# Interval constants over more steps, Newton steps in the quiet part of the weights' cycle, and images placed by eight transfers, in a kernel of three relu-difference convolutions

## The chip, the cores and the metric

The kernel runs on one core of a Trainium2 chip. The metric is the device time of one execution in microseconds (us). One execution was also taken by the hardware profiler; all times of single instructions below come from it.

## What is computed

The reference is a chain of four layers on x (4 images, 32 x 32 pixels, 16 channels, float32), each with a group norm in front and a sum behind it. Layers 0, 1 and 3 are the same convolution-like layer with their own weights, and layer 2 is a dynamic program over intervals:

```python
def conv(inputs, M, W, G):      # layers 0, 1, 3
    first = jnp.einsum('ijyx,byxc->bijc', Msq, inputs)
    shifted = ...               # a 3x3 convolution with own filters for each output pixel (i, j)
    diff = jax.nn.relu(inputs[:, None, None, :, :, :] - shifted)
    second = jnp.einsum('ijyx,bijyxc->bijc', Wsq, diff)
    return first - second

def intervals(a, ...):          # layer 2
    r = [interval_pooling(a, 'max'), interval_pooling(a, 'min')]
    f = dp_step(r, r, W0, b0)                      # max over k of sigmoid(f[i,k] Wf + r[k,j] Wr + b)
    f = dp_step([f, r], r, W1, b1)
    return sigmoid([f, r] @ W2 + b2)[:, :-1, 1:]

for layer in (conv0, conv1, intervals, conv3):
    x = x + layer(group_norm(x))
```

For each output pixel (i, j) and each filter, a whole image of 1024 pixels is convolved, cut at zero, and summed with the weights of that pixel. This is nearly all of the work.

## The kernel before, in words

**Phases and steps.** The four images are two pairs (g = 0, 1). A phase is one pair in one of the three convolution layers, in the order (0, 0), (1, 0), (0, 1), (1, 1), (0, 2), (1, 2), where the second number counts the convolutions. So phases alternate between the pairs, and what has to happen to one pair between two layers (norm, intervals, new operands) is done beside the matmuls of the other pair. A phase has 8 chunks of 128 output pixels, a chunk 16 filters x 2 images = 32 steps, so there are 256 steps in a phase and 1536 in all. One step (first_part and second_part, L678 and L702) is one filter of one image for 128 output pixels and 1024 image pixels:

- TensorE: matmuls into one pair of PSUM banks (L663). The float32 values are split into three parts, and the products of the parts are summed: first the products with ib and ia, then, after ScalarE has scaled the sum in place (L699), those with iyz and im. ia, ib, iyz and im9 are the operands made from the image.
- VectorE: minimum with zero times the weights WT, summed along the row (L716, into the tile junk). It is the last reader of the bank pair. There are four bank pairs, so TensorE starts on a pair again when the L716 of four steps earlier is done.

second_part of a step is issued after first_part of the step that follows. [...]the order is written out by hand, and no scheduler moves anything.

**The weights' cycle.** prep_parts (L221) is a generator that the conv loop calls once per step (`next(parts)`, L754). It prepares one unit (4 filters) of split weights in eight steps. Written by the step number modulo 8: at 1 VectorE makes the upper part (L204, tile upper_w); at 2 ScalarE takes a half for W9 (L176); at 3 GpSimd subtracts (L238) and adds (L239), ScalarE scales (L237); at 4 GpSimd adds and copies (L242, L244, L246) and ScalarE copies (L241); at 5 GpSimd subtracts the identity from the next unit (L215, prep), for which its raw weights must have landed; at 6 nothing; at 7 SyncE issues two transfers of parts (L252) and the load of the raw weights of the unit after the next (L111, 768 KB); at 0 nothing. What the generator yields says for what else a step is good: IDLE at 5, 6, 7, 0 and 1; CALM at 6, 7 and 0.

**What runs beside.** `behind` (L769) is the generator of everything else. The conv loop takes one stretch of it at a time: `yield n` asks for n steps until the next stretch, `yield IDLE` and `yield CALM` wait for a step of that kind (L763 to L765). Its order is:

- phase 0: rest_of_start (L905, the operands of the second image and the norm of the first pair), zeros(1), constants (L462: the mask and small weights of the interval layer, loaded as wv and written by GpSimd as blocks, L476, and the memset of rt, L483);
- phases 3 and 4, ahead of the last convolution of each pair and beside matmuls of the other: interval_layer (L501). It has its group norm (tile names with _i), four transposes (L530), scans (L549), the products left and right_side (L573, L588), and two dynamic steps which end with transfers of s to r, a part of tables (L632); left("l2") at L641 reads r after the last of them;
- then before_conv (L383): the group norm (tile names with _c), a transpose (L390), eight writes to the DRAM tile xs (L396), 24 reads into the tile raw (L407), the split of each of two images on GpSimd (L281) with ScalarE (L285), the half of im (L176), `place` (L291) with its transfers into ia (L299) and ib (L301) through SyncE's queue, and `difference` into iyz (L289);
- after the second pair of layers 0 and 1, and at the end: the first terms (L432).

The group norm (L334) takes sums on VectorE, with `gap` steps between its parts, and then has a block of small operations on GpSimd that follow one another: L326, three times L328 to L331 (Newton steps for an inverse root), and L376, which writes the normed values. They stand in GpSimd's queue between the weights' operations. The norm of the interval layer has gap 2; that of a conv 4, or 1 in the last layer.

**The operands.** temp holds both split parts, ty and tz, of both halves of both images. place copies quarters of it (32 partitions, L195) to the partitions that the matmuls need: per half, four transfers of 32 x 496 to ia and two of 32 x 512 to ib, so twelve for one image, ia ahead of ib.

Of the kernel before, what the change touches and what calls it, by code (L numbers as in the profile page):

```python
# [45 lines left out]
def net_kernel(ctx: ExitStack, tc: tile.TileContext, x, xq, xi, convs, iv_w, iv_b, out):  # L46
# [131 lines left out]
    def halve_rest(dst, src, mask):  # L178
        nc.vector.scalar_tensor_tensor(
            dst, src, mask[:, 0:1], dst.bitcast(F32), op0=ALU.mult, op1=ALU.add  # L180
        )
# [87 lines left out]
        halve_rest(units[u][3][:, at:to], raws[u][:, 2, at:to], low_p)  # L269

    def halves(temp, b):
        v = temp.rearrange("p (k s b n) -> p k s b n", k=2, s=2, b=GB)
        return v[:, 0, :, b], v[:, 1, :, b]

    def split(eng, g, b, temp, name, pause=IDLE):
# [11 lines left out]
    def difference(eng, g, b, s, temp):  # L287
        ty, tz = (v.bitcast(F32)[:, s] for v in halves(temp, b))
        eng.tensor_tensor(iyz[g][:, s, b], ty, tz, ALU.subtract)  # L289

    def place(g, b, temp):  # L291

        ty, tz = (v.bitcast(F32) for v in halves(temp, b))
        da, db = (v[g].bitcast(F32)[:, :, b] for v in (ia, ib))
        for h, (lo, hi) in enumerate(QUARTERS):
            for s in range(2):
                at = HW if s == h else 0
                for to, src in ((lo, ty), (hi, tz)):
                    nc.sync.dma_start(da[to, s, :LAST], src[lo, s, at : at + LAST])  # L299
            for to, src in ((lo, ty), (hi, tz)):  # L300
                nc.sync.dma_start(db[to], src[hi])  # L301
        yield 1


# [26 lines left out]
            nc.gpsimd.tensor_tensor(y, y, t, ALU.mult)  # L331
        return y

    def group_norm(g, name, dst, gap):  # L334


        def sums(src):
            nc.vector.tensor_reduce(
                part[:, : GC // 2], src.rearrange("p t (g s) -> p g t s", s=2), axis=AX.XY, op=ALU.add
            )  # L340

        def totals(name):

            turned = work.tile([P, 32], F32, tag="turned", name=f"turned_{name}")
            nc.vector.transpose(turned, part)
            by_quarter = work.tile([32, 4], F32, tag="by_quarter", name=f"by_quarter_{name}")
            for q in range(4):
                nc.vector.tensor_reduce(
                    by_quarter[:, q : q + 1], turned[32 * q : 32 * q + 32], axis=AX.X, op=ALU.add
                )  # L350
            yield gap
            total = work.tile([P, 32], F32, tag="total", name=f"total_{name}")
            for q in range(4):
                nc.vector.tensor_reduce(
                    total[32 * q : 32 * q + 32, 0:1], by_quarter, axis=AX.X, op=ALU.add
                )
            yield gap
            whole = work.tile([P, 32], F32, tag="whole", name=f"whole_{name}")
            nc.vector.transpose(whole, total[:, 0:1].to_broadcast([P, 32]))
            return whole[:, : GC // 2]  # L360

        sums(X[g])
        yield gap
        m = yield from totals(f"m{name}")
        mean = work.tile([P, GC // 2], F32, tag="mean", name=f"mean_{name}")
        nc.gpsimd.tensor_scalar_mul(mean, m, 1.0 / (2 * NP))
        xc = work.tile([P, NT, GC], F32, tag="xc", name=f"xc_{name}")
        nc.gpsimd.tensor_tensor(pair_view(xc), pair_view(X[g]), spread(mean), ALU.subtract)
        sq = work.tile([P, NT, GC], F32, tag="sq", name=f"sq_{name}")
        nc.gpsimd.tensor_tensor(sq, xc, xc, ALU.mult)  # L370
        yield 4
        sums(sq)
        yield gap
        v = yield from totals(f"v{name}")
        rstd = inverse_root(v, name)
        nc.gpsimd.tensor_tensor(pair_view(dst), pair_view(xc), spread(rstd), ALU.mult)  # L376
        yield 6

    xns = {}
    part = const.tile([P, 32], F32, name="part")  # L380
# [2 lines left out]
    def before_conv(g, layer):  # L383
        xn = work.tile([P, NT, GC], F32, tag="xn", bufs=2, name=f"xn_{g}_{layer}")
        xns[g] = xn
        yield from group_norm(g, f"c{g}{layer}", xn, 1 if layer == 2 else 4)

        nc.vector.transpose(  # L390
            xt[g][:, :, 1 : 1 + H], xn
        )
        inner = xs[g][:, :, WP : WP + H * WP].rearrange("p h (t r n) -> p h r t n", r=ROWS, n=WP)
        for r in range(ROWS):
            for h in range(2):
                nc.sync.dma_start(  # L396
                    inner[:, h, r], xt[g][GC * r : GC * (r + 1), :, HW * h : HW * h + WP]
                )
        yield 2
        xsv = xs[g].rearrange("(b c) h n -> c h b n", b=GB)  # L400
        for slot, row, tap in [
            (slot, row, tap) for slot in range(2) for row, tap in enumerate(TAPS[slot])
        ] + [(2, row, 8) for row in range(4)]:
            for h in range(2):
                off = tap // 3 * WP + tap % 3
                r0 = 64 * h + C * row
                nc.sync.dma_start(  # L407
                    raw[r0 : r0 + C, slot ^ h if slot < 2 else 2, :, :RUN], xsv[:, h, :, off : off + RUN]
                )
            yield 1  # L410
        yield 6 if layer == 2 else 12
        temp = big.tile([P, 8192], F32R, tag="big", name=f"temp_{g}{layer}")[:, :TEMP]
        for b in range(GB):
            yield from split(nc.gpsimd, g, b, temp, f"{g}{layer}")
            yield IDLE
            halve(image(im9[g][:, b], HW), image(raw[:, 2, b], WP), low_x)
            yield from place(g, b, temp)
            for s in range(2):
                difference(nc.gpsimd, g, b, s, temp)
            yield 1  # L420
            halve_rest(image(im9[g][:, b], HW), image(raw[:, 2, b], WP), low_x)
            yield 4

    def load_first_terms(layer):
        mt = big.tile([P, NT, 4, 256], F32, tag="big", name=f"MT_{layer}")
# [36 lines left out]
    def constants():  # L462
# [18 lines left out]
            )  # L481

        nc.gpsimd.memset(rt, 0.0)  # L483
        yield 1


        for k, hidden, name in ((0, None, "f0"), (3, 2, "f1"), (6, 5, "f2")):
# [7 lines left out]
        for k, name in ((1, "r0"), (4, "r1")):  # L495
            t = const.tile([P, NQ * GB, C], F32, name=name)
            for q in range(NQ):
                blocks(t[:, q * GB : (q + 1) * GB, :], k, mask2, GB)
            iv[name] = t.rearrange("p k c -> p (k c)")
            yield 1  # L500
    def interval_layer(g):  # L501

        R = 2 * GC
# [19 lines left out]
        yield 1  # L523
        nc.gpsimd.memset(r[:R, :, 0:1], 0.0)
        nc.gpsimd.memset(r[:R, H:], 0.0)
        yield from group_norm(g, f"i{g}", xi, 2)

        raw = one[:GC].rearrange("p (j t r) -> p r t j", j=H, r=ROWS)
        for row in range(ROWS):
# [108 lines left out]
        yield from right_side("r1", iv["r1"])  # L638
        ftp = left("l1", iv["f1"])
        yield from step("b", ftp, bv[:, 1:2])  # L640
        z = left("l2", iv["f2"])  # L641
        y = ivp.tile([P, QI, H], F32, tag="y", name=f"y_{g}")
        nc.scalar.activation(y, z[:, :, 1:], AF.Sigmoid, bias=bv[:, 2:3])
# [125 lines left out]
    def behind(phase):  # L769
        g, layer = phases[phase]  # L770
        if phase == 0:
            yield from rest_of_start()
            nc.sync.dma_start(X[1], x[1])
            zeros(1)
            yield 1
            yield from constants()
        if phase + 1 < len(phases):
            g1, layer1 = phases[phase + 1]
# [126 lines left out]
    def rest_of_start():  # L905
# [12 lines left out]
        halve_rest(image(im9[0][:, 1], HW), image(raw[:, 2, 1], WP), low_x)  # L918
        prep_plain_rest(1)
        yield 2  # L920
        temp = first.bitcast(F32R)[:, used : used + TEMP]
        for b in range(GB):
            yield from split(nc.vector, 0, b, temp, "00", 1)
            yield from place(0, b, temp)
# [91 lines left out]
```

## Time and profile before

| what | value |
|---|---|
| median of 3 runs | 2479.14 us (2476.86 to 2479.35) |
| the profiled execution | 2478.91 us |
| its span on the core | 2477.1 us |
| L716, VectorE | 1536 of 1224 ns, with 83 ns more to read the sum |
| L699, ScalarE | 1520 of 1008 ns |
| L238, L239, L242, GpSimd | 190 each of 1300 ns |
| L215, GpSimd | 190 of 1052 ns |
| raw weights, L111 | 190 transfers of 768 KB, 7.1 us to landing |
| ia from temp, L299 | 80 transfers of 62 KB, 5.6 us to landing |
| ib from temp, L301 | 40 transfers of 128 KB, 4.4 us to landing |

PE is TensorE's matmuls, PEld its weight loads, DVE is VectorE, ACT ScalarE, POOL GpSimd and SP SyncE. A line of a timeline has the start in us, the duration in us, the engine, the line of the kernel, the operation, what is written and read with partitions x elements, and in brackets how long the engine had been idle before it and who ended that. A line of the waits has who waited for whom, the sum in us, how often, and the longest.

### The profile page before, as it was taken

The page shows a single profiled execution, that of the slowest core. Times are in us where ns is not written, and L with a number is a line of the kernel's source. Part 1 is how long each engine was busy: PE and PEld are TensorE (multiplying, and loading weights), DVE is VectorE, ACT ScalarE, POOL GpSimd, SP SyncE. Part 2 cuts the span into 40 slices and gives each one's busy share as a digit, 9 for nine tenths or more (in the row PEclk, how much of TensorE's full clock was granted, in tenths as well). Part 3 has the DMA queues.
Part 4 walks back from the last instruction along what each step waited for, and adds up shares of the span by engine and source line. Part 5 has one row for each costly group of instructions (what it writes and reads, how often), then busy time and mean ns, then how long its engine had stood idle before and what let it go on. Part 6 is the DMA issues. An engine that isn't in the chain of part 4 may idle for free. (4 is left out here: it accounts for less than half of the span.)

```text
span 2477.1 us, 58166 instructions
## 1 busy us (share of the span) xinstructions
PE 2457.9 (99%) x21906; PEld 2072.9 (84%) x21906; DVE 2077.0 (84%) x3637; ACT 1871.4 (76%) x2159; POOL 1589.7 (64%) x1857
## 2 busy tenths in 40 slices
PE   8999999999999999999999999999999999999999
PEld 5998888888888888888888898888889888888887
DVE  9888878888888888878888888888888888788887
ACT  3778767787777778767777777777777787677776
POOL 4767545676565667555567776776777675555552
PEclk9999999999999999999999999999999999999999
DMA  6457654475444467644454454674445476554442
GB/s 198 128 156 191 188 144 134 131 195 149 135 142 137 137 168 194 190 112 136 137 145 129 126 142 132 174 171 130 129 135 141 119 197 186 154 148 137 137 137 54
DMA packets 97674, 366.92 MB, mean 148 GB/s; under 512 B 26480, under 2 KB 31472, under 8 KB 97392
## 3 DMA queue, kind: packets, MB, share of 16 engines
q1 hardware_dynamic: 96832, 362.79, 53.5%
q8 instruction: 172, 2.82, 0.5%
q14 instruction: 110, 0.90, 0.1%
q10 hardware_dynamic: 432, 0.39, 0.0%
q0 software_dynamic: 128, 0.02, 0.0%
HBM read 199.78 MB, written 1.02 MB: 81 GB/s over the span
## 5 line engine op out<-in xcount | busy, mean ns | idle before, releaser
L716 DVE SCALAR_TENSOR_TENSOR junk<-pc,WT 128x1024 f32<-128x1024 f32 x1536 | 1879.6, 1224 | 353.5 <-PE pc L663 303.8
L699 ACT ACTIVATE pc<-pc 128x1024 f32<-128x1024 f32 x1520 | 1532.2, 1008 | 563.8 <-PE pc L663 530.4
L663 PE MATMUL pc<-ib,parts 64*128 64x512 f32 x6080 | 950.2, 388 | 4.3 <-DVE junk L716 3.0
L663 PE MATMUL pc<-iyz,parts 64*128 64x512 f32 x6080 | 947.2, 387 | 2.3 <-ACT pc L699 1.6
L663 PE MATMUL pc<-ia,parts 64*128 64x496 f32 x6080 | 924.8, 379 | 0.0
L663 PEld LDWEIGHTS pc<-ib,parts 64*128 64x128 f32 x6080 | 582.4, 184 | 109.8 <-DVE junk L716 9.6
L663 PEld LDWEIGHTS pc<-ia,parts 64*128 64x128 f32 x6080 | 585.4, 184 | 106.0
L663 PEld LDWEIGHTS pc<-iyz,parts 64*128 64x128 f32 x6080 | 583.5, 184 | 92.6 <-ACT pc L699 7.3
L663 PE MATMUL pc<-im,W 64*128 64x496 f32 x3072 | 603.2, 384 | 0.0
L238 POOL TENSOR_TENSOR parts<-raw,upper_w 128x512 fp32r<-128x512 f32 x190 | 247.0, 1300 | 497.6 <-DVE upper_w L204 413.1
L663 PEld LDWEIGHTS pc<-im,W 64*128 64x128 f32 x3072 | 296.6, 184 | 56.9 <-issue 3.4
L244 POOL CAST parts<-parts 32x512 fp32r<-32x512 f32 x380 | 231.6, 609 | 39.3 <-ACT parts L241 20.8
L242 POOL TENSOR_TENSOR parts<-parts 128x512 fp32r<-128x512 f32 x190 | 247.0, 1300 | 1.6 <-ACT parts L237 1.5
L246 POOL CAST parts<-upper_w 32x512 fp32r<-32x512 f32 x380 | 233.1, 613 | 22.8
L239 POOL TENSOR_TENSOR W<-W,raw 128x512 fp32r<-128x512 f32 x190 | 247.4, 1302 | 0.4 <-ACT W L176 0.3
L215 POOL TENSOR_TENSOR raw<-raw,ident 128x512 f32<-128x512 f32 x190 | 199.8, 1052 | 73.7 <-DMA raw<-in_g 45.8
L176 ACT ACTIVATE W<-raw,low_w 128x512 fp32r<-128x512 f32 x190 | 136.2, 717 | 1.7 <-DMA raw<-in_g 1.6
L716 DVE DVE_READ_ACCUMULATOR junk<-pc,WT 128x1 f32 x1536 | 127.9, 83 | 0.0
L237 ACT ACTIVATE parts<-upper_w 128x512 fp32r<-128x512 f32 x190 | 118.9, 626 | 7.7 <-DVE upper_w L204 7.5
L241 ACT CAST parts<-upper_w 128x512 fp32r<-128x512 f32 x190 | 116.4, 613 | 0.0
L731 POOL TENSOR_SCALAR acc<-acc 128x32 f32<-128x32 f32 x40 | 15.6, 391 | 136.8 <-DVE junk L716 134.7
L204 DVE TENSOR_SCALAR upper_w<-raw 128x512 int32<-128x512 int32 x190 | 82.4, 433 | 19.0 <-POOL raw L215 18.6
(152 smaller groups left out, 470.4 us busy)
## 6 DMA issues: line engine op xcount, KB each, us to landing
raw<-in_g SPq DMA_DIRECT2D x190, 768.0 KB, 7.1
parts<-parts SPq DMA_DIRECT2D x380, 384.0 KB, 5.0
WT<-in_w SPq DMA_DIRECT2D x48, 512.0 KB, 4.7
MT<-in_mt SPq DMA_DIRECT2D x24, 512.0 KB, 7.3
raw<-xs SPq DMA_DIRECT2D x120, 71.8 KB, 4.1
ib<-temp SPq DMA_DIRECT2D x40, 128.0 KB, 4.4
ia<-temp SPq DMA_DIRECT2D x80, 62.0 KB, 5.6
ib<-first SPq DMA_DIRECT2D x8, 128.0 KB, 2.4
```

The lines of the kernel that those rows point to most:

```text
L176: nc.scalar.activation(dst, src, AF.Copy, scale=mask[:, 1:2])
L215: eng.tensor_tensor(raws[u][:, s, at:to], raws[u][:, s, at:to], pick[s][:, f0 + at : f0 + to].unsqueeze(2).to_broadcast([P, to - at, P]), ...
L237: nc.scalar.activation(WD, high, AF.Copy, scale=-EPS)
L238: nc.gpsimd.tensor_tensor(WL, w8, high, ALU.subtract)
L239: nc.gpsimd.tensor_tensor(W9, W9.bitcast(F32), src[:, 2], ALU.add)
L241: nc.scalar.copy(WU, high)
L242: nc.gpsimd.tensor_tensor(WD, WD.bitcast(F32), WL.bitcast(F32), ALU.add)
L244: nc.gpsimd.tensor_copy(WU[hi], WL[lo].bitcast(F32))
L246: nc.gpsimd.tensor_copy(WL[lo], high[hi])
L663: nc.tensor.matmul(ps[:, h, at : at + n], lhsT=w[r], rhs=v[r] if n == NH else v[r][:, :n], start=first and k == 0, stop=k == len(pairs) - ...
L699: nc.scalar.activation(ps, ps, AF.Copy, scale=1.0 + EPS)
L716: nc.vector.scalar_tensor_tensor(junk, ps.rearrange("p h n -> p (h n)"), 0.0, chunks[n], op0=ALU.min, op1=ALU.mult, accum_out=accs[phase][ ...
```

## The change

The kernel after differs in four places.

- **place and its position.** One image is placed by eight transfers: the four to ib first (32 x 2 x 512, as before), then four to ia (32 x 2 x 496), each for both halves at once; they read temp through a view with a pitch, for which temp is now the whole tile. In before_conv the order is now split, half of im, difference, two steps, rest of im, two steps, place. Before, place came right behind the half of im.
- **constants.** Six steps instead of one ahead of them, four instead of one after the memset of rt, and a step after each of the blocks of r0 and r1. What follows in phase 0, the conv norm of the second pair among it, comes 14 steps later.
- **The norm of the interval layer.** Its gap is 1 instead of 2, it waits for a CALM step ahead of the GpSimd block, and 4 instead of 6 steps follow it.
- **yield 2 ahead of left("l2").** What follows it, the conv norm of the last layer among it, comes two steps later.

In steps of their phase: the block of the interval norm comes at a step that is 6 modulo 8 (before 1); that of the conv norm of the second pair in layer 0 at 2 (before 4); those of the two conv norms in the last layer at 2 (before 0). The other conv norms keep their places.

```diff
     def place(g, b, temp):
-        ty, tz = (v.bitcast(F32) for v in halves(temp, b))
+        parts = halves(temp.bitcast(F32)[:, :TEMP], b)
         da, db = (v[g].bitcast(F32)[:, :, b] for v in (ia, ib))
+        for lo, hi in QUARTERS:
+            for to, src in zip((lo, hi), parts):
+                nc.sync.dma_start(db[to], src[hi])
         for h, (lo, hi) in enumerate(QUARTERS):
-            for s in range(2):
-                at = HW if s == h else 0
-                for to, src in ((lo, ty), (hi, tz)):
-                    nc.sync.dma_start(da[to, s, :LAST], src[lo, s, at : at + LAST])
-            for to, src in ((lo, ty), (hi, tz)):
-                nc.sync.dma_start(db[to], src[hi])
+            for k, to in enumerate((lo, hi)):
+                at = (2 * k * GB + b) * NH + HW * (1 - h)
+                pitch = GB * NH + HW * (2 * h - 1)
+                src = temp.bitcast(F32)[lo, at : at + 2 * pitch].rearrange("p (s n) -> p s n", s=2)
+                nc.sync.dma_start(da[to, :, :LAST], src[:, :, :LAST])
         yield 1
...
-    def group_norm(g, name, dst, gap):
+    def group_norm(g, name, dst, gap, pause=None, behind=6):
...
         v = yield from totals(f"v{name}")
+        if pause is not None:
+            yield pause
         rstd = inverse_root(v, name)
         nc.gpsimd.tensor_tensor(pair_view(dst), pair_view(xc), spread(rstd), ALU.mult)
-        yield 6
+        yield behind
...
-        temp = big.tile([P, 8192], F32R, tag="big", name=f"temp_{g}{layer}")[:, :TEMP]
+        temp = big.tile([P, 8192], F32R, tag="big", name=f"temp_{g}{layer}")
         for b in range(GB):
             yield from split(nc.gpsimd, g, b, temp, f"{g}{layer}")
             yield IDLE
             halve(image(im9[g][:, b], HW), image(raw[:, 2, b], WP), low_x)
-            yield from place(g, b, temp)
             for s in range(2):
                 difference(nc.gpsimd, g, b, s, temp)
+            yield 2
+            halve_rest(image(im9[g][:, b], HW), image(raw[:, 2, b], WP), low_x)
+            yield 2
+            yield from place(g, b, temp)
             yield 1
-            halve_rest(image(im9[g][:, b], HW), image(raw[:, 2, b], WP), low_x)
-            yield 4
...
         nc.gpsimd.memset(rt, 0.0)
-        yield 1
+        yield 4
...
             for q in range(NQ):
                 blocks(t[:, q * GB : (q + 1) * GB, :], k, mask2, GB)
+                yield 1
             iv[name] = t.rearrange("p k c -> p (k c)")
-            yield 1
...
-        yield from group_norm(g, f"i{g}", xi, 2)
+        yield from group_norm(g, f"i{g}", xi, 1, CALM, 4)
...
         yield from step("b", ftp, bv[:, 1:2])
+        yield 2
         z = left("l2", iv["f2"])
...
             zeros(1)
-            yield 1
+            yield 6
             yield from constants()
...
-        temp = first.bitcast(F32R)[:, used : used + TEMP]
+        temp = first.bitcast(F32R)[:, used:]
```

More of the change, by code (lines that the diff above doesn't have):

```diff
@@ L271, in halves @@
     def halves(temp, b):
-        v = temp.rearrange("p (k s b n) -> p k s b n", k=2, s=2, b=GB)
+        v = temp[:, :TEMP].rearrange("p (k s b n) -> p k s b n", k=2, s=2, b=GB)
         return v[:, 0, :, b], v[:, 1, :, b]
```

## The prediction

> **What bounds the kernel now.** I read the shares of the page first, then what TensorE waited for, then the timelines around each gap.
>
> ```profile
> PE 2457.9 (99%) x21906; PEld 2072.9 (84%) x21906; DVE 2077.0 (84%) x3637; ACT 1871.4 (76%) x2159; POOL 1589.7 (64%) x1857
> ```
>
> TensorE is busy for all but 19 us of a span of 2477.1 us. A step (one hidden feature of one image) goes by each 1.567 us while nothing is late (the starts of two L699 six steps apart, counted in the trace), and no part of the change touches a matmul. So only the idle time can be won or enlarged. Of it some 14 us lie at the two ends; that a 99% share still hides gaps, and restarts after gaps, is shown by the distances between steps: summed over all steps they exceed 1.567 us by 45.2 us, of which 21.4 us are three runs of first-term matmuls (real work). The rest is my list of stalls.
>
> ```profile
> PE pc L663 <- DVE junk L716: 3.0, 4, 1.1
> ...
> PE pc L663 <- DMA ib<-first: 1.0, 1, 1.0
> PE ps_l L573 <- DMA tables<-s_b: 0.6, 2, 0.4
> ```
>
> The first row is the pattern of all large stalls: TensorE waits for DVE (L716 frees a PSUM bank), and DVE waits for GpSimd (POOL). The first interval norm shows how:
>
> ```profile
> 1276.19 0.67 POOL L376 TENSOR_TENSOR xi<-xc_i,root_y_i 128x256 f32<-128x256 f32 x1
> 1276.82 1.29 POOL L238 TENSOR_TENSOR parts<-raw,upper_w 128x512 fp32r<-128x512 f32 x1
> ...
> 1283.38 1.04 POOL L215 TENSOR_TENSOR raw<-raw,ident 128x512 f32<-128x512 f32 x1
> ```
>
> ```profile
> 1281.89 0.07 DVE L716 DVE_READ_ACCUMULATOR junk<-pc,WT 128x1 f32 x1
> 1284.45 0.43 DVE L204 TENSOR_SCALAR upper_w<-raw 128x512 int32<-128x512 int32 x1 [2.49 <-POOL raw L215]
> 1284.79 1.22 DVE L716 SCALAR_TENSOR_TENSOR junk<-pc,WT 128x1024 f32<-128x1024 f32 x1
> ```
>
> L326 to L376 took 4.70 us (1272.12 to 1276.82) in front of L238, POOL then worked 7.63 us without a gap up to L204, and DVE, whose next L204 stands ahead of L716 in its queue, stood for 2.49 us. Four bank pairs let DVE be late by about 1.78 us: here L204 was 2.62 us behind its turn and TensorE idled 0.80 us; at 112.95 us 2.82 and 1.06; at 99.7 us 2.08 and 0.33; at 1567.5 us 1.59 and 0.06. So **idle = lateness of L204 less 1.78 us**. Afterwards steps stay a little long while DVE catches up (its 1.365 us per step against 1.567); the first interval norm costs 1.885 us in all, the second 1.909.
>
> [...]L716 at 1284.79 us stood behind L204. [...]L281 on 128x512 takes 1254 ns on POOL and 679 on DVE (1.85 times), L289 1386 and 910. So POOL's weights work, 7.4 us of every 12.5, is what a Newton block of 4.7 us pushes back. [...]in the SP queue one L299 group issued at 1607.89 us held the queue for 5.26 us.
>
> **The change part by part**, against the profiled execution (2478.91 us; span 2477.1 and 1.81 around it; 0.23 below the median of the runs shown, 2479.14).
>
> *Constants.* Steps between zeros, the memset of rt and the blocks grow, so that wv has landed before L476. Now POOL waits there with L242 queued behind:
>
> ```profile
> 108.19 0.23 POOL L476 TENSOR_TENSOR f<-wv,mask 64x32 f32<-64x32 f32 x1 [2.46 <-DMA wv<-in_iv_w]
> ```
>
> The stall that follows (1.06 us idle at 114.68) has an excess of 1.219+0.134+0.059 = 1.41 us. Gone: **-1.41**. Bounds -1.41 to -0.7 (if a block lands beside a POOL peak).
>
> *The conv norm behind the constants.* It shifts by 14 steps, from 84 to 98 of the first phase. Weights units have a cycle of eight steps: POOL is loaded at 3, 4 and 5 (L238 to L246, L215) and free from 6 to 2. Step 84 was 4 mod 8 and cost nothing. Step 98 is 2 mod 8: Newton comes directly in front of L238 of step 99. The same norm of the first pair, with the same gap, stood at step 41 (1 mod 8) and made L204 2.08 us late. One step later is 2.08+1.57 = 3.65 us; idle 1.87, restart 0.3: **+2.2**. Bounds +1.5 to +2.6.
>
> *Interval norms.* With CALM they wait for steps 6, 7 or 0 mod 8: they come at 782 and 1038 (6 mod 8) instead of 785 and 1041 (1 mod 8). Newton's 4.7 us are three steps, over before step 3. The transposes L530 move to 786 to 792; DVE has 0.2 us of room per step for their 0.64 us each, as now. Both stalls go: -1.885-1.909 = **-3.79**. Bounds -3.8 to -3.0. Behind it the scans wait for a calm step anyway.
>
> *yield 2 ahead of left("l2").* Two more steps let tables<-s_b land before L573. The two excesses there are 1.56 and 1.68 us, where the l1 product, which doesn't wait, has 0.82: -0.74-0.86, I take **-1.4**; bounds -1.6 to -0.6 (the bare idle, 0.24+0.36).
>
> *What this moves.* The two conv norms of the last layer now come two steps later: Newton at 962 and 1218 (2 mod 8) instead of 960 and 1216 (0 mod 8). At 960 it is already just covered:
>
> ```profile
> 1566.03 0.08 DVE L716 DVE_READ_ACCUMULATOR junk<-pc,WT 128x1 f32 x1
> 1567.49 0.43 DVE L204 TENSOR_SCALAR upper_w<-raw 128x512 int32<-128x512 int32 x1 [1.38 <-POOL raw L215]
> ```
>
> 1.59 us late now; two steps later 1.59+3.13 = 4.7 us, so 2.95 idle and 0.2 to 0.3 of restart: 3.2, less 0.40 and 0.32 that they cost now: +2.8+2.9 = **+5.7**. Bounds +3.5 to +6.2. Behind it the late unit also delays L252 and L111 (step 967) in SP's queue; the eight xs writes (L396, step 968) now stand behind that raw load, were ahead of it before, and the reads L407 behind them, then the raw load of step 975. If that lands after its turn, L204 of 985 is late by 2.0 to 2.4: 0.2 to 0.9 each, and the images' L281 behind a late L215 on POOL 0.3 more. Both norms: **+1.2**, bounds 0 to +3.
>
> *Images placed by eight transfers, ib first, later.* At the start TensorE waited 0.96 us (excess 1.252) for ib<-first, which was issued after the ia transfers of its half; it is now issued first: **-1.25**, bounds -1.25 to 0. Later the place transfers come four steps behind the split, so behind the raw load, not ahead of it. At 1644 us a raw load came late (POOL L215 idle 7.36 us) and DVE stood:
>
> ```profile
> 1645.03 0.43 DVE L204 TENSOR_SCALAR upper_w<-raw 128x512 int32<-128x512 int32 x1 [3.34 <-POOL raw L215]
> ```
>
> Its excess is 1.755+0.127 = 1.88. One cause is a queue in which transfers of place wait for one another; the same place elsewhere had no such stall, so it may be chance. I take **-1.88**, bounds -1.88 to 0. Four transfers fewer per image save some 0.6 us of issue each on SP, which is not the bound: 0. POOL's L289 moves ahead of place, which is only an order; L281 of the second image now waits for transfers of the first: covered by POOL's free steps, else up to 1 us late, below the 1.78: 0.
>
> **Sum.** -1.41-3.79-1.4-1.25-1.88 = -9.73; +2.2+5.7+1.2 = +9.1. Net -0.6: 2478.91-0.6 = **2478.3**. A measurement of this kernel can tell about 0.2% (5 us) from no change, so this is no change.
>
> **The rivals.**
> - *The moved Newtons are covered* (chance 0.15). For it: POOL is busy only 64% and the norm at 960 costs 0.4. Against: the rule above, from four stalls. Then only the gains stay: 2478.91-9.73 = 2469.2, up to 2474.5 if half of the losses remain.
> - *Slower by late raw loads* (0.10). The late L252, then xs writes behind the raw load, make two raw loads per last-layer norm as late as the one at 1644 us: four times 1.88 = 7.5 in place of the 1.2: 2478.3+6.3 = 2484.6. It decides from the point where a raw load lands over 1.78 us past the turn of its L215 plus what POOL has free. For it: the 7.36 us of POOL idle at 1643.95. Against: raw loads land after a median of 7.1 us and have some twelve.
> - *Place does nothing* (0.17): the stalls at 50 and 1644 us stay or reappear elsewhere, 2478.3+1.25+1.88 = 2481.4. For it: only one of the image placements showed a stall. Against: at the start the order of issue is changed in the right way.
>
> **How the numbers follow.** The forecast has 0.58 (2475 to 2482). The range takes in the third case and goes a little into the first two, which leaves 0.12 below and 0.08 above: 2473.0 to 2483.5. Against 2479.14 the bounds of 0.2% are 2474.2 and 2484.1: faster 0.14, same 0.78, slower 0.08.
>
> **What would show it.** TensorE's gaps at 50, 115, 1285 and 1697 us gone; L238 of the interval units at its turn. New: L204 waiting for POOL for about 3.3 us near 185 us and over 4 us near 1567 and 1980 us, with L376 ending just before L238. It would be wrong if L204 comes in time there, if raw loads are late in the last layer, or if the gap at 1644 us is still there.

## The result and the profile after

The changed kernel takes 2493.06 us (median of 6 runs, 2491.87 to 2497.78), the kernel before beside it 2478.55 us (6 runs, 2476.86 to 2479.35). The ratio is 1.0061 with a 95% interval of 1.0048 to 1.0074: it is slower by 14.5 us, where I had forecast 2478.3 and a range up to 2483.5. The profiled execution took 2492.37 us, its span is 2490.7 us.

The shares of the page and the waits of TensorE, of the kernel after:

```profile
PE 2462.6 (99%) x21906; PEld 2062.1 (83%) x21906; DVE 2079.4 (83%) x3637; ACT 1871.5 (75%) x2159; POOL 1588.4 (64%) x1857
```

```profile
PE pc L669 <- DVE junk L722: 11.2, 8, 3.0
PE pc L669 <- ACT pc L705: 4.2, 6, 1.9
```

In the kernel before, the second of these rows was:

```profile
PE pc L663 <- ACT pc L699: 1.6, 2, 1.2
```

The shares hardly move. The waits do: TensorE waits 11.2 us for DVE in place of 3.0, and 4.2 us for ACT in place of 1.6. The rows for ib<-first and s_b, which the prediction showed, are gone. (L663, L699 and L716 of before are L669, L705 and L722 now, L396 and L407 are L400 and L411.) As TensorE's busy time also grew by 4.7 us, though its matmuls are the same, waits alone are not all.

I listed again by how much the distance from one step to the next exceeds 1.567 us; this is called the excess below. Summed over all steps it is 60.1 us after and 46.1 before (the prediction's 45.2 comes out if a step is taken 0.0006 us longer), so 14.1 us more, which is the difference of the spans (13.6) but for 0.5. It stands in a few places:

| place | before | after | change | predicted |
|---|---|---|---|---|
| start, 44 to 51 us | 1.77 | 0.82 | -0.95 | -1.25 |
| constants, 113 us | 1.41 | 0 | -1.41 | -1.41 |
| interval norms | 3.79 | 0.48 | -3.32 | -3.79 |
| left("l2"), above the 0.82 of l1 | 1.60 | 0 | -1.6 | -1.4 |
| conv norm of pair 1, layer 0 | 0 | 2.27 | +2.27 | +2.2 |
| conv norms of the last layer | 0.71 | 9.75 | +9.04 | +5.7 |
| images of phase 0 | 0.39 | 2.80 | +2.4 | 0 |
| images of phase 4 | 0.41+1.88 | 4.86 | +2.6 | -1.88+0.6 |
| images of phase 5 | 0.42 | 5.57 | +5.2 | +0.6 |

"Images" are the steps in which the operands of the next phase are read back from xs, split and placed. Here and below the images of phase 0 are those prepared in phase 0 (for phase 1), while those of phases 4 and 5 are named by the phase that uses them: they are prepared in phases 3 and 4, behind the two norms of the last layer. "Newton" is short for the GpSimd block of a norm.

First what went as forecast, the unit behind the first interval norm, in GpSimd's timeline after:

```profile
1273.17 0.68 POOL L380 TENSOR_TENSOR xi<-xc_i,root_y_i 128x256 f32<-128x256 f32 x1
...
1280.36 1.04 POOL L215 TENSOR_TENSOR raw<-raw,ident 128x512 f32<-128x512 f32 x1
1285.20 1.30 POOL L238 TENSOR_TENSOR parts<-raw,upper_w 128x512 fp32r<-128x512 f32 x1 [3.80 <-DVE upper_w L204]
```

L215 is done 3.80 us ahead of the L238 that follows, so POOL waits for DVE and not DVE for POOL: the stall of 1.9 us is gone.

Then the first norm of the last layer. VectorE's timeline, and the table of stretches (columns after the times: busy us of PE, PEld, DVE, ACT and POOL with their instructions, the granted clock, the DMA share, GB/s):

```profile
1565.37 0.44 DVE L394 STREAM_TRANSPOSE xt<-xn 128x256 f32<-128x256 f32 x1
1569.71 0.43 DVE L204 TENSOR_SCALAR upper_w<-raw 128x512 int32<-128x512 int32 x1 [3.90 <-POOL raw L215]
```

```profile
1568.50:1571.30 2.80, 0.00 (x0) 0.00 (x0) 1.57 (x3) 1.13 (x2) 2.12 (x3) 1.00 0.68 136
1571.30:1572.90 1.60, 1.57 (x8) 1.29 (x10) 1.35 (x3) 0.95 (x2) 1.60 (x3) 0.51 0.88 250
1572.90:1574.50 1.60, 1.60 (x12) 1.23 (x10) 1.11 (x2) 1.01 (x1) 1.53 (x2) 0.50 0.78 207
1574.50:1576.00 1.50, 1.50 (x16) 1.26 (x14) 1.23 (x2) 0.29 (x1) 1.38 (x3) 0.92 0.99 303
```

TensorE idles 2.90 us, near the 2.95 worked out. What I had not seen is in the column of the clock: when it starts again, its clock is 0.51 and 0.50 in two stretches of 1.60 us, after 1.00 in the one before. The step from 1571.33 us is 1.54 us longer than 1.567, with PE busy all the time; the same at 1987.98 (clock 0.50 from 1987.8 to 1991.1 us). That is where "busy" time grew.

Last, the images. SyncE's queue, before and then after (the duration covers a row of issues, the waits among them too):

```profile
1563.65 3.78 SPq L396 DMA_DIRECT2D xs<-xt  x8
1567.60 1.11 SPq L252 DMA_DIRECT2D parts<-parts  x2
1568.75 1.20 SPq L111 DMA_DIRECT2D raw<-in_g  x1
1570.06 10.35 SPq L407 DMA_DIRECT2D raw<-xs  x14
1580.58 1.11 SPq L252 DMA_DIRECT2D parts<-parts  x2
...
1582.97 8.75 SPq L407 DMA_DIRECT2D raw<-xs  x10
1591.88 1.11 SPq L252 DMA_DIRECT2D parts<-parts  x2
```

```profile
1568.58 1.11 SPq L252 DMA_DIRECT2D parts<-parts  x2
1569.80 1.13 SPq L111 DMA_DIRECT2D raw<-in_g  x1
1570.98 7.65 SPq L400 DMA_DIRECT2D xs<-xt  x8
1579.94 4.67 SPq L411 DMA_DIRECT2D raw<-xs  x10
1584.78 1.11 SPq L252 DMA_DIRECT2D parts<-parts  x2
1585.99 1.22 SPq L111 DMA_DIRECT2D raw<-in_g  x1
1587.26 11.59 SPq L411 DMA_DIRECT2D raw<-xs  x14
1599.01 1.11 SPq L252 DMA_DIRECT2D parts<-parts  x2
```

Before, the eight writes to xs take 3.78 us and are through when the raw load is issued. After, they stand behind it and take 7.65 us. Issue and landing of each, from the trace:

```
raw<-in_g (L111)  issued 1569.80  landed 1578.31
xs<-xt, 1st       issued 1570.98  landed 1578.61
xs<-xt, 7th       issued 1575.85  landed 1579.81
xs<-xt, 8th       issued 1578.33  landed 1579.99
raw<-xs, 1st      issued 1579.94  landed 1582.12
```

The eighth write behind the raw load is issued 0.02 us after that load has landed, and the small ones land with it, up to 7.6 us after issue. Why the eighth: in the trace SyncE's transfers signal eight semaphores in turn, and the eighth write waits for the one that the raw load signals (number 107). The first read of xs comes only with the last writes, 14 of the reads then hold the queue for 11.59 us, and the last L252 shown is issued at 1599.01 us in place of 1591.88. Of these 7.1 us, 3.8 are TensorE's own delay by then, mostly from the stall at the norm (its step 983 starts at 1590.27 in place of 1586.49), and 3.3 are left for the queue. The raw load behind this L252, issued at 1600.22, takes 9.9 us to land (8.5 before), and GpSimd and ScalarE wait for it until 1610.14 us:

```profile
1610.22 0.72 ACT L176 ACTIVATE W<-raw,low_w 128x512 fp32r<-128x512 f32 x1 [1.53 <-DMA raw<-in_g]
```

ScalarE's L705 stands behind this L176, TensorE idles 1.13 us for it and 1.08 us more for DVE.

### The profile page after: what moved, and what is told of

Its sections match the earlier page's. It is cut to its first block, busy times and chain, and to the rows that moved or that the text cites. A ratio compares the mean times of both kernels' runs of the same rounds, so it can differ in the third digit from the quotient of the medians.

```text
span 2490.7 us, 58090 instructions
## 1 busy us (share of the span) xinstructions
PE 2462.6 (99%) x21906; PEld 2062.1 (83%) x21906; DVE 2079.4 (83%) x3637; ACT 1871.5 (75%) x2159; POOL 1588.4 (64%) x1857
## 4 chain that ended last, share of the span: by engine, by line
PE 92%; POOL 3%; DMA 2%; DVE 1%; issue 1%; ACT 1%; SPq 0%; POOLq 0%; DVEq 0%; ACTq 0%
PE pc L669 91%; DMA raw<-in_g 1%; DVE junk L722 1%; PE pf L444 1%; ACT pc L705 0%; POOL raw L215 0%; POOL parts L244 0%; POOL parts L242 0%; POOL parts L246 0%; POOL parts L238 0%; POOL iyz L289 0%; DMA parts<-parts 0%; SPq L411 0%; PE ps_l L578 0%; ACT temp L285 0%
## 5 line engine op out<-in xcount | busy, mean ns | idle before, releaser
L722 DVE SCALAR_TENSOR_TENSOR junk<-pc,WT 128x1024 f32<-128x1024 f32 x1536 | 1879.4, 1224 | 354.4 <-PE pc L669 301.6
L705 ACT ACTIVATE pc<-pc 128x1024 f32<-128x1024 f32 x1520 | 1532.1, 1008 | 568.5 <-PE pc L669 536.3
L669 PE MATMUL pc<-ib,parts 64*128 64x512 f32 x6080 | 950.5, 388 | 11.8 <-DVE junk L722 11.2
L669 PE MATMUL pc<-iyz,parts 64*128 64x512 f32 x6080 | 947.0, 387 | 4.7 <-ACT pc L705 4.2
L669 PE MATMUL pc<-ia,parts 64*128 64x496 f32 x6080 | 924.5, 379 | 0.0
L669 PEld LDWEIGHTS pc<-ib,parts 64*128 64x128 f32 x6080 | 580.3, 184 | 122.2 <-DVE junk L722 19.2
L669 PEld LDWEIGHTS pc<-ia,parts 64*128 64x128 f32 x6080 | 582.4, 184 | 110.1
L669 PEld LDWEIGHTS pc<-iyz,parts 64*128 64x128 f32 x6080 | 580.5, 184 | 99.8 <-ACT pc L705 11.3
L669 PE MATMUL pc<-im,W 64*128 64x496 f32 x3072 | 602.3, 384 | 0.0
L238 POOL TENSOR_TENSOR parts<-raw,upper_w 128x512 fp32r<-128x512 f32 x190 | 247.7, 1304 | 540.3 <-DVE upper_w L204 438.3
L669 PEld LDWEIGHTS pc<-im,W 64*128 64x128 f32 x3072 | 295.2, 184 | 59.0 <-issue 3.6
L215 POOL TENSOR_TENSOR raw<-raw,ident 128x512 f32<-128x512 f32 x190 | 198.0, 1042 | 66.3 <-DMA raw<-in_g 43.0
L176 ACT ACTIVATE W<-raw,low_w 128x512 fp32r<-128x512 f32 x190 | 136.2, 717 | 5.2 <-DMA raw<-in_g 5.1
L722 DVE DVE_READ_ACCUMULATOR junk<-pc,WT 128x1 f32 x1536 | 127.4, 83 | 0.0
L204 DVE TENSOR_SCALAR upper_w<-raw 128x512 int32<-128x512 int32 x190 | 85.7, 451 | 30.0 <-POOL raw L215 29.7
```

Source lines behind the costliest of these rows:

```text
L176: nc.scalar.activation(dst, src, AF.Copy, scale=mask[:, 1:2])
L215: eng.tensor_tensor(raws[u][:, s, at:to], raws[u][:, s, at:to], pick[s][:, f0 + at : f0 + to].unsqueeze(2).to_broadcast([P, to - at, P]), ...
L238: nc.gpsimd.tensor_tensor(WL, w8, high, ALU.subtract)
L669: nc.tensor.matmul(ps[:, h, at : at + n], lhsT=w[r], rhs=v[r] if n == NH else v[r][:, :n], start=first and k == 0, stop=k == len(pairs) - ...
L705: nc.scalar.activation(ps, ps, AF.Copy, scale=1.0 + EPS)
L722: nc.vector.scalar_tensor_tensor(junk, ps.rearrange("p h n -> p (h n)"), 0.0, chunks[n], op0=ALU.min, op1=ALU.mult, accum_out=accs[phase][ ...
```

## The experiments

Theory A, formed on these traces: the loss has two roots. Newton stands ahead of L238, and, apart from that, the move of the norms put the writes to xs behind L252 and L111 in SyncE's queue. Theory B: the new place and its position make the stalls at the images. Theory C: these stalls follow from the late weights' unit, not from an order. Each comparison is with the kernel before on the same chip, whose median was 2478.79 us for the first four runs below, 2479.74 for old place, place alone, old constants and the first late units, and 2480.12 for the other four. Excesses and waits are those of each kernel's one profiled execution.

**Calm norms.** The block of the three moved conv norms waits for a quiet step:

```diff
+        moved = layer == 2 or (g, layer) == (1, 0)
-        yield from group_norm(g, f"c{g}{layer}", xn, 1 if layer == 2 else 4)
+        yield from group_norm(g, f"c{g}{layer}", xn, 1 if layer == 2 else 4, CALM if moved else None)
```

> The changed kernel, with a wait for a CALM step ahead of the GpSimd block of the three conv norms that the change moved (pair 1 of layer 0, both pairs of the last layer): Newton at 6 modulo 8 in place of 2, and with it the xs writes at 4 in place of 0, ahead of L252 and L111. Theory A (Newton ahead of L238, and xs writes behind the raw load in SP's queue): the three stalls of 2.27, 4.89 and 4.86 us go, and the stalls behind them at the images of phases 0, 4 and 5 as well (2.4, 4.5 and 5.2 us): 2493.1-24 = 2469. Theory B (the stalls at the images come from the new place and its position): only the 12.0 us of the norms go: 2481.

Measured: 2473.15 us (13 runs), ratio to before 0.9976 (0.9967 to 0.9984). All three norm stalls are gone, and the images cost 1.1, 1.4 and 2.7 us in phases 0, 4 and 5 in place of 2.8, 4.9 and 5.6. It is 4 us above theory A's figure and 8 below B's. The quiet position alone turns the change from a loss into a gain. SyncE's queue in it:

```profile
1569.20 3.79 SPq L401 DMA_DIRECT2D xs<-xt  x8
...
1575.05 1.11 SPq L252 DMA_DIRECT2D parts<-parts  x2
1576.20 1.31 SPq L111 DMA_DIRECT2D raw<-in_g  x1
```

The writes are ahead again and take 3.79 us. As this run moves Newton and the writes at once, the next three take them apart.

**xs ahead.** Newton stays ahead of L238; the writes, and with them the reads, the split and place, come two steps earlier.

```diff
+        moved = layer == 2 or (g, layer) == (1, 0)
-        yield from group_norm(g, f"c{g}{layer}", xn, 1 if layer == 2 else 4)
+        yield from group_norm(g, f"c{g}{layer}", xn, 1 if layer == 2 else 4, None, 4 if moved else 6)
```

> The changed kernel, with 4 in place of 6 steps behind the three moved conv norms: Newton stays ahead of L238 (2 modulo 8), and the xs writes come at 6 in place of 0 modulo 8, so ahead of L252 and L111 in SP's queue. Theory A (order in SP's queue): the norms' stalls stay, those at the images go (about 12 us): 2481. Theory C (the stalls at the images come from the lateness of the weights' unit itself, whatever the order): no change, 2493. Theory B (place): no change, 2493.

Measured: 2482.42 us (20 runs), ratio 1.0013 (1.0006 to 1.0019). The images cost 0.7, 0.5 and 0.4 us, the norms 2.3, 3.4 and 5.0. This is theory A's case to 1.4 us: a late Newton with the writes ahead makes no stall at the images, so B and C are out as their main cause.

```profile
1561.82 3.78 SPq L401 DMA_DIRECT2D xs<-xt  x8
1567.33 1.11 SPq L252 DMA_DIRECT2D parts<-parts  x2
...
1581.44 1.10 SPq L252 DMA_DIRECT2D parts<-parts  x2
```

L252 is issued at 1567.33 us, late as in the changed kernel (1568.58), but the one after it at 1581.44 and not at 1584.78.

**Without yield 2.** The last layer's norms are where they were.

```diff
-        yield 2
         z = left("l2", iv["f2"])
```

> The changed kernel without the yield 2 ahead of left(l2): the two norms of the last layer come at 0 modulo 8 as in the kernel before, xs writes at 6. Theory A: both norm stalls (4.89 and 4.86) shrink to 0.4 and 0.3, the stalls at the images of phases 4 and 5 shrink by 4.5 and 5.2, and the wait of left(l2) is back (1.6): 2493.1-9.1-9.7+1.6 = 2476. Theory B (place): the images' stalls stay: 2485.6.

Measured: 2479.20 us (12 runs), ratio 1.0004 (0.9995 to 1.0012). The norms of the last layer cost 0.43 and 0.35 us, the images of phases 4 and 5 0.5 and 1.1. It is 3 us above theory A's figure: those of phase 0, which the edit does not touch, cost 4.5 us here and 2.8 in the changed kernel. So one yield is worth 14.1 us of the 14.5 (0.4 against the kernel before is left without it), though the 1.6 us of left("l2") were gained by it.

**xs behind.** From the kernel without yield 2, the writes two steps later, and with them all that stands behind them (reads, split and place):

```diff
-        yield from group_norm(g, f"c{g}{layer}", xn, 1 if layer == 2 else 4)
+        yield from group_norm(g, f"c{g}{layer}", xn, 1 if layer == 2 else 4, None, 8 if layer == 2 else 6)
```

> As the run without yield 2, but with 8 in place of 6 steps behind the two norms of the last layer: Newton at 0 modulo 8 (no stall there), xs writes at 0 modulo 8, behind L252 and L111. Theory A (order in SP's queue alone makes the images' stalls): about 9 us more than the run without yield 2: 2485. Theory C (the late unit makes them): the same as the run without yield 2: 2476.

Measured: 2489.55 us (4 runs), ratio 1.0042 (1.0025 to 1.0059), so 10.4 us more than without the edit, with Newton in a place where the norms cost 0.39 and 0.38 us. The move by two steps alone, with no late Newton, makes the stalls at the images (5.6 and 5.7 us, of which 1.54 in phase 4 is a fallen clock). SyncE's queue without yield 2, and then with the writes behind:

```profile
1565.61 3.78 SPq L400 DMA_DIRECT2D xs<-xt  x8
1569.56 1.11 SPq L252 DMA_DIRECT2D parts<-parts  x2
```

```profile
1569.84 1.11 SPq L252 DMA_DIRECT2D parts<-parts  x2
1571.06 1.14 SPq L111 DMA_DIRECT2D raw<-in_g  x1
1572.24 8.08 SPq L400 DMA_DIRECT2D xs<-xt  x8
```

The raw load landed at 1580.00 us here, and the eighth write was issued at 1580.01. As reads, split and place move along, this run does not part the writes from them; that the writes' place is what counts is read from the queue.

**Old place in the calm kernel.** Calm norms, with place and its position as before the change (the diff of place and of before_conv taken back).

> The kernel with calm norms (first run), but images placed as before: twelve transfers, right behind the half of im, difference behind them, temp cut as before. Theory B1 (the new place is worth what I forecast, the start's 1.25 and a stall of a late raw load as at 1644 us): 2473.2+1.25+1.9 = 2476. Theory B2 (it is worth the start's 0.7 at most, and the raw loads' lateness is a matter of where they stand in the queue): 2473 to 2474. Below 2472 it would cost time.

Measured: 2473.06 us (10 runs), ratio 0.9973 (0.9963 to 0.9982), as the calm kernel with the new place (0.9976). There the eight transfers and their delay are worth nothing that this can tell; B2 holds.

**Place alone.** The kernel before with the new place and position.

> The kernel before, with nothing but the new place and its position. Theory B1: the stalls at 50 us (0.7 to 1.25) and 1644 us (1.9) go: 2478.8-2.6 = 2476. Theory B2: 2478 to 2479. Theory B (the new position delays raw loads and makes the stalls at the images): over 2483.

Measured: 2477.47 us (20 runs), ratio 0.9993 (0.9986 to 0.9999): 1.7 us at the middle of the interval. The steps of the start lose 0.74 us of excess, the stall of a late raw load (1.88 us at 1644 us before) is absent, and 0.2 and 0.7 us come at other images of phases 4 and 5: nearer to B1 than to B2. The two kernels with late units below place as before and have the stall at 1644 us too, with 0.9 and 2.4 us; the runs with the new place don't have it. So it has no fixed size, and it is absent with the new place in every profile. The gain at the start is less sure: two other profiles with the old place, old place in the calm kernel and the first late units, have 1.08 us there and no wait for ib<-first, as much as most with the new one (1.0 to 1.1). So part or all of it can be chance.

**Old constants.** The changed kernel with the three spreads of constants taken back:

```diff
-            yield 6
+            yield 1
             yield from constants()
...
         nc.gpsimd.memset(rt, 0.0)
-        yield 4
+        yield 1
...
                 blocks(t[:, q * GB : (q + 1) * GB, :], k, mask2, GB)
-                yield 1
             iv[name] = t.rearrange("p k c -> p (k c)")
+            yield 1
```

> The changed kernel with the constants spread as before: the conv norm of pair 1 in layer 0 is back at step 84 (4 modulo 8), its xs writes at 90 (2 modulo 8), ahead of L252. Theory A: its stall (2.27) and those at the images of phase 0 (2.4) go, the constants' stall (1.41) is back: 2493.1-3.3 = 2489.8. Without the link to the images: 2492.2.

Measured: 2490.52 us (4 runs), ratio 1.0045 (1.0028 to 1.0062). The norm's stall is gone, the images of phase 0 cost 1.2 us in place of 2.8, and the constants' stall is back with 1.07 us. So the spread of the constants gained 1.1 to 1.4 us and lost 3.9 through what stands behind it.

**Late units.** What does an idle TensorE cost beyond the idle? In the kernel before, rows of small products on GpSimd ahead of L238:

```diff
+            for _ in range(late.get(u, 0)):
+                nc.gpsimd.tensor_tensor(pad[:, :16], pad[:, :16], pad[:, 16:32], ALU.mult)
             nc.gpsimd.tensor_tensor(WL, w8, high, ALU.subtract)
```

> The kernel before, with added work that delays GpSimd: in seven units of weights in a quiet stretch of phase 1 a row of small products (17, 19, 21, 22, 23, 25, 21 of about 0.305 us) stands ahead of L238, as a Newton block does. By idle = delay - 1.8 of POOL's own room - 1.78 of the banks', TensorE should idle 1.6, 2.2, 2.8, 3.1, 3.4, 4.0 and 2.8 us. Theory K (an idle of about 2.9 us lets the clock fall to 0.5 and costs 1.55 us more): the stretches from about 2.8 show the slow step, those of 1.6 and 2.2 don't; in all about 2478.8+20+1.5+4 times 1.55 = 2506. Rival (the slow step in the changed kernel came from something else on the chip): restarts of 0.2 everywhere, 2500.

Measured: 2479.88 us (one run). The rows made one idle of 0.96 us (the row of 23, at 750 us) where seven of 1.6 to 4.0 were expected. The row of 17 began at 584.72 us, when POOL had nothing to do, and was over before it mattered. I had counted POOL's room wrongly: its chain starts when upper_w is there (1 modulo 8), two steps before the program issues L238, and a row that waits for nothing runs in POOL's own idle time ahead of it. Newton can't, since it waits for VectorE's sums. So this run tells nothing of the clock.

**Late units, tied to upper_w.** The first product of a row reads upper_w, and the rows are longer:

```diff
+            for k in range(late.get(u, 0)):
+                by = high[:, :16] if k == 0 else pad[:, 16:32]
+                nc.gpsimd.tensor_tensor(pad[:, :16], pad[:, :16], by, ALU.mult)
```

> As the run with late units, but the first small product of each row reads upper_w, so that a row can't run in POOL's idle time ahead of it, and the rows are longer: 25, 27, 28, 29, 30, 31 and 33 products of 0.305 us. From upper_w to the next one's turn POOL has 12.5-8.2 = 4.3 us of room: by idle = delay - 4.3 - 1.78 TensorE should idle 1.5, 2.2, 2.5, 2.8, 3.1, 3.4 and 4.0 us. Theory K: up to about 2.2 us the restart costs 0.2, above about 2.9 us the clock falls to 0.5 and it costs 1.55 more. Rival: restarts of 0.2 everywhere. The time: 2478.8+19.5+1+(3 to 5) times 1.55 = 2505, or 2500.

Measured: 2508.93 us (one run). TensorE idled 1.87, 1.75, 2.05, 2.35, 2.98, 2.96 and 3.54 us, within 0.5 of the rule. Its clock fell after 2.05 (1.73 us more), 2.35 (1.53) and 3.54 (1.73, beginning late in the first step), and not after 1.87, 1.75, 2.98 and 2.96, where the steps behind cost 0.13. Two of the stretches, 2.05 and 2.98 us of idle, from their starts:

```profile
683.70 0.80 PE L669 MATMUL pc<-ib,parts 64*128 64x512 f32 x4 [2.05 <-DVE junk L722]
684.28 1.04 PE L669 MATMUL pc<-ia,parts 64*128 64x496 f32 x4
```

```profile
767.90 0.73 PE L669 MATMUL pc<-ib,parts 64*128 64x512 f32 x4 [2.98 <-DVE junk L722]
768.47 0.62 PE L669 MATMUL pc<-ia,parts 64*128 64x496 f32 x4
```

Four matmuls of ia span 1.04 us in the first and 0.62 in the second; the granted clock of the 1.5 us behind the idle is 0.68 and 1.00. The fall is real and apart from anything else in the changed kernel, but it has no threshold at 2.9 us, which theory K assumed.

**One step in place of two.**

```diff
-        yield 2
+        yield 1
         z = left("l2", iv["f2"])
```

> The changed kernel with one step in place of two ahead of left(l2): Newton of the last layer's norms at 1 modulo 8 (idle 4.8-1.57-1.78 = 1.4 us, no fall of the clock, so about 1.8 in place of 4.9 us each), xs writes at 7, in the same step behind L252 and L111. If order in SP's queue makes the images' stalls: they stay (9.6 us), 2493.1-6.2+0.5 = 2487. If they need the lateness of Newton at 2: 2478.

Measured: 2490.69 us (4 runs), ratio 1.0041 (1.0027 to 1.0055). The norms cost 2.3 and 2.0 us (idle 1.40 and 1.36, as worked out), the images 6.5 and 5.1: they stay, with a Newton that is late by 1.6 us less. Here even the transfers of parts (L252) are late: TensorE waits 0.83 and 1.26 us for them at 1592 and 1593 us. It is 4 us above my figure, as phases 0 (4.7) and 4 cost more than in the changed kernel. Against the run with the writes ahead, whose writes are issued at 6 modulo 8, this is one step, and the step in which L252 and L111 are issued lies between: the images go from 0.5 and 0.4 us to 6.5 and 5.1.

**Two tries at a better kernel.** The first adds to the calm norms a quiet place for the first norm (step 46 in place of 41), four in place of six steps ahead of the constants, and splits that begin where they did before in the weights' cycle. The second also issues the reads of layers 0 and 1 one a step:

```diff
                 nc.sync.dma_start(
                     raw[r0 : r0 + C, slot ^ h if slot < 2 else 2, :, :RUN], xsv[:, h, :, off : off + RUN]
                 )
-            yield 1
+                if h or layer < 2:
+                    yield 1
```

> The kernel with calm norms, and also: a wait for a CALM step ahead of the first pair's norm in layer 0 (its Newton at step 46, 6 modulo 8, in place of 41), four in place of six steps ahead of the constants (so that the next norm comes at 102), and the split of the images later by two steps in the last layer and six for pair 1 of layer 0, so that it begins at 2 and at 4 modulo 8 as in the kernel before. The stall at 98 us (0.66) goes; if the stalls of 0.8 at the images of phases 0, 4 and 5 come from where the split stands in the weights' cycle, 2.4 more go: 2473.1-3.1 = 2470. If they come from the transfers alone: 2472.5.

> As the run before it, and in layers 0 and 1 the 24 reads of the image from xs are issued one a step in place of two (eight or six in place of twelve steps follow them). If the late raw loads of phases 0 to 2 (1.4 us at 521 us in the kernel with calm norms) come from reads that wait in SP's queue ahead of L252 and L111, that stall goes: 1 to 1.5 us under the run before it; otherwise the same.

Measured: 2473.52 us (10 runs), ratio 0.9974 (0.9965 to 0.9984), and 2471.59 us (5 runs), ratio 0.9966 (0.9954 to 0.9979). The first is no better than the calm norms: the stall at 98 us is gone, but the images of phases 4 and 5 cost 1.9 and 3.8 us in its profile, so where the split stands in the cycle was not their cause. The late raw load at 521 us (1.4 us in the calm kernel) is down to 0.3 us in the first and gone in the second, so reads one a step aren't shown to be its cure. In phase 5 of the second one late raw load is left (1.55 us of idle, and a fallen clock, 4.0 us in all; the images of that phase cost 5.2). The second has the lowest median of all; its interval overlaps that of the calm norms.

Over all profiles, with the writes to xs ahead of or behind L252 and L111, the images cost:

| kernel | phase 0 | phase 4 | phase 5 |
|---|---|---|---|
| before | ahead, 0.4 | ahead, 2.3 | ahead, 0.4 |
| after | behind, 2.8 | behind, 4.9 | behind, 5.6 |
| calm norms | ahead, 1.1 | ahead, 1.4 | ahead, 2.7 |
| xs ahead | ahead, 0.7 | ahead, 0.5 | ahead, 0.4 |
| without yield 2 | behind, 4.5 | ahead, 0.5 | ahead, 1.1 |
| xs behind | behind, 4.8 | behind, 5.6 | behind, 5.7 |
| old place, calm | ahead, 0.4 | ahead, 1.3 | ahead, 3.6 |
| place alone | ahead, 0.4 | ahead, 0.6 | ahead, 1.1 |
| old constants | ahead, 1.2 | behind, 4.9 | behind, 4.1 |
| late units | ahead, 0.4 | ahead, 1.7 | ahead, 0.4 |
| late units, tied | ahead, 1.7 | ahead, 3.9 | ahead, 1.0 |
| one step | behind, 4.7 | behind, 6.5 | behind, 5.1 |
| first try | ahead, 0.4 | ahead, 1.9 | ahead, 3.8 |
| second try | ahead, 0.4 | ahead, 0.9 | ahead, 5.2 |

Behind costs 2.8 to 6.5 us in all twelve cases. Ahead costs at most 2.7 in 26 of 30, but 3.6 to 5.2 in four, so being ahead is not enough. Two kinds stand out. With the old place, the stall of the late raw load at 1644 us is part of the figure (1.9 of the 2.3 before, 2.4 of the 3.9). And in phase 5 of the four kernels with calm norms, the writes come at 4 modulo 8 and 16 reads follow a raw load in one block. In the run with calm norms:

```profile
1987.59 12.28 SPq L412 DMA_DIRECT2D raw<-xs  x16
```

The next L252 comes at 2000.02 us and the one after it at 2006.59, close together as in the changed kernel (1599.01 and 1604.38). That the block of reads does there what the writes do when behind is likely by these times, but no run shows it alone, and the same block costs 0.9 to 1.9 us in phase 4.

## Why the prediction was wrong

The forecast was 2478.3 us and the time is 2493.06, 14.8 us more. By its steps:

- *Constants, interval norms, left("l2")*: right in place and size, -6.3 together against -6.6. Each interval norm keeps 0.24 us.
- *The start*: -0.95 against -1.25, but partly luck, as the stall there is absent from two profiles with the old place.
- *The conv norm behind the constants*: right, +2.27 against +2.2.
- *The two norms of the last layer*: the mechanism and the idle were right (2.90 and 2.96 us against 2.95). The term "0.2 to 0.3 of restart" failed: the clock fell and the restart cost 1.54 us each time, 2.6 us in all. I took it from stalls of 0.3 to 1.2 us, the longest that the trace of before had, and used it for one of 3 us.
- *What stands behind the norms* was the step that failed: "+1.2, bounds 0 to +3" for the last layer, and nothing for phase 0. Measured by the images' excess, less the stall at 1644 us, it is 4.5+5.2 in phases 4 and 5 and 2.4 in phase 0, 12.0 us in all; the runs with the writes ahead and behind show that it is a cost of order. I had the queue and the order right: the writes behind the raw load, the reads behind the writes, the next raw load behind the reads. The size failed: I priced the end of this chain as one L204 late by 2.0 to 2.4 us, 0.2 to 0.9 us of idle, and 0.3 at the images, without adding up how long each link holds the queue (7.65 us for the writes, 4.67 and 11.59 for the reads), and I counted no wait of ScalarE's L176 for the same load. This step makes 10.8 us of the 14.8, the two norms 3.3. And in phase 0 I looked at where Newton had moved, but not at where the writes had: step 90 to 104 is from 2 to 0 modulo 8, the same crossing as in the last layer.
- *The late raw load at 1644 us*: gone as forecast, and by the new place in the kernel before (place alone). With calm norms, which read the images at other steps, the old place has no such stall either.
- *Side effects of place*, put at 0: 0.2 and 0.7 us with place alone, and no difference in the calm kernel.

The slower rival had the right mechanism, "xs writes behind the raw load", with 0.10 and 7.5 us for the last layer, where 9.7 were measured. Its price was too low, since it took the stall of another place, and its chance too: "raw loads land after a median of 7.1 us and have some twelve" speaks of landing, while the load was late mostly because it was issued late, at 1600.22 in place of 1593.09 us; landing took 1.4 us longer too. The covered rival was wrong where it counts: Newton ahead of L238 is not covered. (Its "up to 2474.5 if half of the losses remain" should be 2473.7, which is 2469.2 and half of 9.1; nothing rests on it.)

What stays open: why the clock falls after one idle of 2.05 us and not after one of 2.98; what decides the 0.4 to 5.2 us that the images cost with the writes ahead; and how much of the cost behind is the writes' and how much that of the reads that move with them.

## What to carry to other kernels

When an edit shifts a stretch of work by a step or two, list every instruction in it, transfers above all, and for each the queue in which it now stands behind something else: here one yield that gained 1.6 us put eight small writes, and the reads that need them, behind a 768 KB load, which cost ten. A cost read from the trace of before holds for waits of the size found there: restarts after 0.3 to 1.2 us of idle cost 0.2 to 0.3 us, those after 2.9 us in the changed kernel cost 1.5. And put blocks that wait for another engine where the engine's own regular work leaves room: a wait for a quiet step turned +14.5 us into -5.6.

## What the runs showed of the hardware

*The clock after an idle TensorE.* Where the granted clock fell, the traces show it at 0.50. The length of the idle alone does not tell whether it falls: it fell after idles of 2.05 and 2.35 us, in a stretch of 1.90 and 1.09 us close together (xs behind), and once where the longest idle was 1.55 us (phase 5 of the second try). Of seven idles of 2.96 to 2.98 us, four made it fall (one in the kernel after, one with xs ahead, two with old constants) and three did not (one with xs ahead, two of the late units). None of nine idles of 1.36 to 2.00 us that stood alone made it fall (phase 0's norm in five kernels, the run with one step, the late units). So equal idles ended differently, and no run here shows why. The cost was 1.54 us each time in the kernel after, and 1.73, 1.53 and 1.73 us in the late units tied to upper_w.

*One queue.* In SyncE's queue a transfer that waits holds up those behind it: in the kernel after the seventh write is issued at 1575.85 us, the eighth, which waits for the raw load, at 1578.33, and the first read only at 1579.94. The cases above are what this costs: eight small writes hold the queue for 3.8 to 4.5 us ahead of a raw load and for 6.4 to 8.1 right behind one, in all fourteen profiles. In the kernel after and in xs behind, the eighth is issued 0.02 and 0.01 us after the load's landing (1578.31 and 1578.33, 1580.00 and 1580.01). This wait is made by the eight semaphores that the program uses in turn, as the operands in the trace of the kernel after show (the raw load signals number 107, and the eighth write waits for it).
